# Reordering the opening of a convolution and attention kernel: loads, second-band inputs and the first phase's keys

## The chip, the core and the metric

The kernel runs on one core of a Trainium2 chip. Five engines work at the same time, each through its own instruction queue in the order of the program: PE (TensorE, matrix products and transposes), ACT (ScalarE, activation functions), DVE (VectorE), POOL (GpSimd) and SP (SyncE, which here only issues DMAs; ACT issues some as well). They wait for each other through semaphores. The metric is the device time of one execution in microseconds (us).

## What is computed

The input `x` has 4 images of 64 x 64 places with 128 channels, all in 32-bit floats. Two layers follow each other:

```python
c1  = conv3x3(elu(x), W1) + b1
c2  = conv3x3(c1, W2) + b2;  a, b = split(c2);  c3 = a * sigmoid(b)
# layer 0: one causal attention head over 4096 tokens, widths 4 and 16, tiled 8 times, then W3
x   = x + c3 + attention0(c3) @ W3 + b3
# layer 1: 16 heads of width 8 over the 4096 tokens, then a gated MLP (128 -> 344 -> 128)
t   = x + (h + ffn(h)),  h = n + attention1(n) @ wo,  n = layernorm(x)
# then 8 experts of 128 x 128, the best two mixed by their softmax weights
out = t + experts(layernorm(t))
```

The second attention is the bulk of the work: for each image and each of the 16 heads a 4096 x 4096 matrix of scores goes through the exponential.

## The kernel before, in words

An image's 4096 tokens are cut into 8 chunks of 512 (`NQ`), and keys into tiles of 128. The image is also seen as 4 bands of 16 rows, two chunks to a band. All engines are wrapped in `InOrder` (line 104), so each executes exactly in the order in which the Python code calls it. Every instruction is issued from line 114, so the profile shows that line everywhere and the groups are told apart by the names of their tiles.

**The stream.** After an opening in which the first image's convolutions begin, one long loop (line 1494) runs the second attention of all images. Each turn issues one step (line 922): 4 score products, 2 exponentials on ACT over 128 x 1024, and the products with the values. Between these the planner inserts pieces of other work, the fillers: the next chunks' and images' convolutions, first attention, layernorms, projections, and the MLP and experts of finished chunks. Fillers are Python generators; a turn usually advances one of them by one or two pieces, chosen from estimated costs.

**Phases of image 0.** The second attention needs keys of all chunks, so image 0 is done in three phases, with 2, 4 and 8 chunks of keys (line 1374). A phase runs over 4 groups of 4 heads; a pair of one group and one chunk of queries is a `Segment`. The first phase has 8 segments of 8 steps. A segment may start when `second`, the number of chunks whose operands are stored in DRAM, has reached the phase's number; otherwise the stream yields `None`, and the turn has no exponentials. Inside `stream` (line 1389), `bring` loads a run's values (`vg`) and a segment's queries (`qx`), for a follower already at the first step of the segment before it; `key_quarter` loads a quarter of a group's keys into one of 4 places in `kx` (the first phase uses place g for group g) and is called when a segment begins; `reload` refills a freed place for a later segment that is ready. A segment whose operands were not brought ahead is `late`: four turns of `None` precede it.

**The opening.** `run_alone` (line 1266) advances five generators in rounds, one piece of each per round, in this order: `convolutions` of image 0, `first_attention`, `second_operands_beside`, `fold_and_spread` (DVE) and `spread_beside` (POOL). The last two turn the 3 x 3 taps into Winograd form for later. Because that takes a while, bands 0 and 1 of image 0 are convolved directly by `first_bands` (line 489): `nine` issues 9 accumulated products per group of 8 rows, in three parts of 3 products, one part per round, all into one PSUM tile `m`. A band has two groups and a short one of a single row for the first layer, then for each of its two chunks a group for the value half and one for the gate half of the second layer; ACT finishes each group.

Their inputs come from `elu(n)` (line 546), which makes chunks up to number n: `neg` = exp on ACT, `pos` in two DVE instructions, a transpose on PE, and a DVE copy into `e_band`. It is a pipeline of three places, so k chunks take k + 2 pieces. Image chunks `xe` have two buffers: chunk n + 2 is loaded after chunk n has been read. `e_band` and `c_band` are two bands each, with a rim of zeros.

Before the rounds begin, line 226 loads the constants (the identity for the transposes among them), line 252 the first two image chunks, lines 253 to 263 the taps and biases on ACT's queue, lines 1289 and 1290 advance the convolution by five pieces, and then the other weights are loaded. Once `first_bands` has ended, `convolutions` makes the POOL terms `row_terms` and `col_terms` (lines 430 and 436; tile `r` shares one buffer with `taps2b`) for its Winograd part. `run_alone` stops when two chunks of second operands are stored, the taps are spread and `first_bands` is over. A layernorm (line 328) runs on DVE, except for its `rs`, a power on POOL.

Of the kernel before, what the change touches and what calls it, by code (L numbers as in the profile page):

```python
# [9 lines left out]
FP = mybir.dt.float32  # L10
FR = mybir.dt.float32r
AF = mybir.ActivationFunctionType
# [3 lines left out]
P = 128  # L16
# [110 lines left out]
def fast_path(ctx: ExitStack, tc: tile.TileContext, a: dict, where: dict, out: bass.AP, verdict):  # L127
# [95 lines left out]

    n_fast = where["tri"][1]
    consts = const.tile([P, n_fast], FP, name="f_consts")
    sp.dma_start(out=consts, in_=a["consts"][:, :n_fast])
    k_of = {name: consts[:, lo:hi] for name, (lo, hi) in where.items() if hi <= n_fast}
    ident = k_of["ident"]

# [3 lines left out]
    def load_x(b, c, tag):  # L233
        t = chunk(tag)
        sp.dma_start(out=by_k(t), in_=tb_x[b][:, 4 * c : 4 * c + 4, :])
        return t
# [8 lines left out]
    def taps(src, room=None):  # L245
# [3 lines left out]
            act.dma_start(out=t[:, i], in_=src[i].rearrange("kw i o -> i kw o"))  # L249
        return t  # L250

    first_x = [load_x(0, c, "xe") for c in range(2)]
    taps1 = taps(a["L0_conv_W1"])
    taps2a = taps(a["L0_conv_W2"][:, :, :, :C])
    b1 = const.tile([P, 1], FP, name="f_b1")
    act.dma_start(out=b1, in_=a["L0_conv_b1"].unsqueeze(1))
    b2 = const.tile([P, 2], FP, name="f_b2")
    act.dma_start(out=b2, in_=a["L0_conv_b2"].rearrange("(h p) -> p h", p=P))
    half_b2 = const.tile([P, 2], FP, name="f_half_b2")
    half_b2a = half_b2[:, 0:1]  # L260
    taps2b = taps(
        a["L0_conv_W2"][:, :, :, C:], row_tile()[:, : 9 * C].rearrange("p (i j o) -> p i j o", i=3, j=3)
    )


    v0 = const.tile([P, NT, SLOT], FP, name="f_v0")
# [8 lines left out]
    for band in (*e_band, *c_band):  # L275
        pool.memset(band[:, :, 0:1], 0.0)
        pool.memset(band[:, :, IMG + 1 :], 0.0)

    acc = ps_o.tile([P, QB], FP, tag="acc", name="acc")
    dve.memset(acc, 0.0)  # L280
    pool.tensor_scalar(half_b2, b2, 0.5, None, ALU.mult)

    seen = const.tile([P, 4, B], FP, name="f_seen")

# [204 lines left out]
    def first_bands(st, elu):  # L489


        def nine(taps, band, y, n):
            ps = rows(m_tile()[:, : n * IMG])
            for m in range(9):
                i, j = divmod(m, 3)
                pe.matmul(
                    ps,
                    lhsT=taps[:, i, j, :],
                    rhs=band[:, y + i : y + i + n, j : j + IMG],
                    start=m == 0,  # L500
                    stop=m == 8,
                )
                if m in (2, 5):
                    yield 0.0, "stop"
            return ps

        for r in range(2):
            here, there = e_band[r], e_band[1 - r]
            c_here = c_band[r]
            if r == 0:  # L510
                pool.memset(here[:, 0, :], 0.0)
                pool.memset(c_here[:, 0, :], 0.0)
            else:
                yield from elu(5)
                pool.tensor_copy(c_here[:, 0, :], c_band[0][:, 16, :])
            for band, y, n, to in (
                (here, 0, 8, slice(1, 9)),
                (here, 8, 8, slice(9, 17)),
                (there, 0, 1, slice(17, 18)),
            ):  # L520
                ps = yield from nine(taps1, band, y, n)
                act.activation(c_here[:, to, 1 : IMG + 1], ps, AF.Identity, bias=b1)
                yield 0.0, "stop"
            st.c3 = wk.tile([P, 2 * QB], FP, tag="c3", bufs=2, name="c3")
            for h in range(2):
                c3, gate = st.c3[:, h * QB : (h + 1) * QB], chunk("sd", "gate")
                ps = yield from nine(taps2a, c_here, 8 * h, 8)
                act.activation(rows(c3), ps, AF.Identity, bias=half_b2a, scale=0.5)
                yield 0.0, "stop"
                ps = yield from nine(taps2b, c_here, 8 * h, 8)  # L530
                act.activation(rows(gate), ps, AF.Tanh, bias=half_b2[:, 1:2], scale=0.5)
                dve.scalar_tensor_tensor(c3, gate, 1.0, c3, ALU.add, ALU.mult)
                st.done.append(c3)
                yield 0.0, "stop"
        st.plain = False

    def tiles(ap):
# [725 lines left out]

    batches = []

    def run_alone(gens, until):

        gens, last = list(gens), {}
        while gens and not (until() and "rounds" not in last.values()):
            for gen in list(gens):  # L1270
                r = next(gen, None)
                while r is not None and r[1] == "held":
                    r = next(gen, None)
                last[gen] = r and r[1]
                if r is None:
                    gens.remove(gen)
                if steps_in:
                    do_step(steps_in.pop(0))
                    finish(1)
                elif undone:  # L1280
                    finish(0)
        while steps_in:
            do_step(steps_in.pop(0))
        finish(0)
        return gens

    Batch(0)

    for _ in range(5):
        next(batches[0].conv)  # L1290

    def weight(name, src, shape):
        w = const.tile(shape, FP, name="f_" + name)
# [92 lines left out]
    jobs = []  # L1386
    now, quiet = [0], [False]

    def stream():
        in_kx, vg_of = [None] * 4, {}  # L1390
        ahead = {}

        def key_quarter(seg, quarter):
            place, what = seg.place(quarter), (seg.b, seg.g, quarter)
            if in_kx[place] != what:
                keys(scratch[seg.b], seg.g, quarter, place)
                in_kx[place] = what

        def bring(seg):

            if seg.run not in vg_of:
                vg_of.clear()
                vg_of[seg.run] = values_of(scratch[seg.b], seg.g, seg.n)
            ahead[seg] = queries(scratch[seg.b], seg.g, seg.c), vg_of[seg.run]

        def reload(at, seg, quarter):

            for later in plan[at + 1 :]:
                quarters = [q for q in range(later.lo // 8, later.hi // 8) if later.place(q) == seg.place(quarter)]
                if quarters:  # L1410
                    if later.ready():
                        key_quarter(later, quarters[0])
                    break

        for at, seg in enumerate(plan):
            now[0] = seg.b
            while not seg.ready():
                yield None
            late = seg not in ahead
            if late:  # L1420
                bring(seg)
            qx, vg = ahead.pop(seg)
            part = []
            for quarter in range(seg.lo // 8, seg.hi // 8):
                key_quarter(seg, quarter)
            for _ in range(4 if late else 0):
                yield None
            follower = plan[at + 1] if at + 1 < len(plan) else None
            over = []
            for kt in range(seg.lo, seg.hi):  # L1430
                if kt in seg.beside:
                    continue
                if kt == seg.lo + 2:
                    seg.jobs = [Beside(seg, n, qx, vg) for n in range(len(seg.beside))]
                    jobs[:] = seg.jobs
                steps_left[seg.b] -= 1

                quiet[0] = kt < seg.lo + 2 and at > 0 and not late
                if seg.lo > 0 and kt == seg.lo + 4:

                    part.append(chunk("part"))
                    sp.dma_start(out=part[0], in_=scratch[seg.b]["p"][seg.g, seg.c])
                yield attention_step(seg.b, seg, kt, 8 * seg.place(kt // 8) + kt % 8, qx, vg, part)
                if follower and follower not in ahead and follower.ready():
                    bring(follower)
                if kt % 8 == 7:
                    over.append(kt // 8)
                if not any(job.kt // 8 in over and job.units < NSLOT for job in seg.jobs):
                    for quarter in over:
                        reload(at, seg, quarter)  # L1450
                    over.clear()
            for job in seg.jobs:
                while job.units < NSLOT:
                    while bank_held[0]:
                        insert()
                    beside_work(1e9)
                    job.piece()
            for quarter in over:
                reload(at, seg, quarter)
# [14 lines left out]
    def spread_beside():  # L1474
# [5 lines left out]
    left = run_alone(  # L1480
        [st.conv, first_attention(0, st), second_operands_beside(0, st), fold_and_spread(), spread_beside()],
        lambda: st.second >= plan[0].n and len(spread_of) == 3 and not st.plain,
    )
    alone[0] = False

# [790 lines left out]
```

## Time and profile before

| What | Value |
|---|---|
| Runs of the kernel | 7969.11, 7976.05, 7983.45 us; median 7976.05 |
| The profiled execution | 7979.66 us, of it 7977.8 us between its first and last instruction (the span) |
| Granted PE clock, mean over the span | 0.992 |
| DMA traffic | 360.96 MB, mean 45 GB/s |

The profile describes one execution. Its page gives busy times by engine, the span in 40 slices of 199 us with the busy share in tenths, and the costliest groups. The timeline lists instructions in order of time, neighbours of one kind merged: start, duration, engine, line, operation, the tile written and the tiles read, the count, and in brackets the idle time of the engine before it with what ended it. `SPq` and `ACTq` are DMA issues. Windows give the busy time of each engine in chosen stretches. The columns of the next lines are the window, its length, busy times with instruction counts, the granted PE clock, the DMA share and GB/s:

```profile
0.00:20.00 20.00, 3.35 (x12) 2.15 (x12) 5.57 (x13) 3.06 (x4) 3.52 (x28) 1.00 0.66 165
20.00:40.00 20.00, 18.24 (x36) 7.59 (x36) 10.57 (x15) 0.69 (x1) 16.07 (x17) 1.00 0.45 116
...
80.00:100.00 20.00, 9.54 (x47) 4.83 (x45) 11.67 (x39) 1.72 (x3) 1.38 (x3) 0.86 0.00 0
100.00:120.00 20.00, 18.53 (x74) 9.82 (x74) 14.38 (x29) 3.88 (x5) 0.00 (x0) 0.79 0.35 121
...
180.00:200.00 20.00, 10.96 (x108) 5.68 (x108) 12.77 (x35) 5.71 (x6) 1.18 (x2) 0.74 0.26 94
200.00:220.00 20.00, 19.28 (x216) 7.35 (x216) 6.00 (x11) 19.65 (x23) 0.00 (x0) 1.00 0.20 62
```

The busy times stand in the order PE, PE weight loads, DVE, ACT, POOL. From 200 us on ACT is busy nearly all the time; before, PE is, except in the first window, from 80 to 100 and from 180 to 200.

### The profile page before, as it was taken

The numbers are of one execution on the slowest core, as the hardware profiler recorded it, in microseconds if no ns is written. First come the engines' busy times: TensorE is split into PE (matmuls) and PEld (weight loads), VectorE is DVE, ScalarE is ACT, GpSimd is POOL, SyncE is SP. The second block draws the span as 40 slices with busy tenths as digits, with TensorE's granted clock in tenths as the row PEclk, the third lists the DMA queues.
The fourth block names the chain that finished last, engine by engine and source line by source line (L and its number), as shares of the span: only waits on it lengthen the run. The fifth ranks groups of instructions, "written<-read, shape, count | busy, mean of one in ns | idle before, by whom it ended". The sixth has DMA issues, their size and how long they took to land.

```text
span 7977.8 us, 237947 instructions
## 1 busy us (share of the span) xinstructions
PE 7760.0 (97%) x103701; PEld 3280.2 (41%) x103701; DVE 4798.3 (60%) x9289; ACT 7661.9 (96%) x8459; POOL 671.5 (8%) x592
## 2 busy tenths in 40 slices
PE   7899999999999999999999999999999999999998
PEld 3333444444444444444444444444444333333334
DVE  4333556462666776666666776666666666666664
ACT  1899999999999999999999999999999999999996
POOL 1201211000022100000001210000000000000000
PEclk9999999999999999999999999999999999999998
DMA  2222011111110111111010011111111111111221
GB/s 71 70 68 69 23 60 33 60 41 53 35 34 15 50 39 50 38 31 43 25 41 29 19 43 43 51 42 34 33 29 52 50 49 53 50 54 50 70 73 38
DMA packets 334834, 360.96 MB, mean 45 GB/s; under 512 B 148211, under 2 KB 224467, under 8 KB 333779
## 3 DMA queue, kind: packets, MB, share of 16 engines
q1 hardware_dynamic: 329763, 343.87, 13.6%
q8 instruction: 814, 13.34, 0.7%
q10 hardware_dynamic: 4016, 1.77, 0.1%
q14 instruction: 241, 1.97, 0.1%
HBM read 209.50 MB, written 136.05 MB: 43 GB/s over the span
## 4 chain that ended last, share of the span: by engine, by line
PE 44%; issue 2%; DVE 2%; ACT 2%; DMA 0%; POOL 0%; SPq 0%; ACTq 0%; DVEq 0%; POOLq 0%
PE acc L114 22%; PE s L114 13%; PE m L114 9%; ACT e L114 1%; DVE ey L114 1%; DVE h L114 0%; DVE em L114 0%; DVE t L114 0%; DVE eg L114 0%; DVE by_e L114 0%; DMA blocks<-d_y 0%; SPq L114 0%; POOL rs L114 0%; DVE f_c_band L114 0%; DVE c L114 0%
## 5 line engine op out<-in xcount | busy, mean ns | idle before, releaser
L114 ACT ACTIVATE e<-s 128x1024 f32<-128x1024 f32 x8256 | 7600.4, 1113 | 111.2 <-PE s L114 106.6
L114 PE MATMUL acc<-e,vg 128*9 128x128 f32 (+3 forms) x61880 | 4278.8, 387 | 1.9 <-DVE at L114 1.8
L114 PE MATMUL s<-qx,f_kx 32*128 32x512 f32 (+1 forms) x16512 | 2556.8, 495 | 88.7 <-ACT e L114 56.4
L114 PEld LDWEIGHTS acc<-e,vg 128*9 128x9 f32 x61880 | 1562.0, 90 | 1777.6 <-issue 1209.5
L114 PEld LDWEIGHTS s<-qx,f_kx 32*128 32x128 f32 (+1 forms) x16512 | 1049.1, 182 | 2068.4 <-ACT e L114 1337.7
L114 DVE SCALAR_TENSOR_TENSOR ey<-ey,eg 128x512 f32<-128x512 f32 x1344 | 940.2, 700 | 31.9
L114 DVE COPY at<-acc 128x512 f32<-128x512 f32 x131 | 90.6, 691 | 597.9 <-PE acc L114 593.4
L114 PE MATMUL m<-v,f_wino 128*32 128x256 f32 x5376 | 420.2, 391 | 12.0 <-POOL v L114 7.3
L114 DVE TENSOR_SCALAR ey<-m 128x512 f32<-128x512 f32 x448 | 307.6, 687 | 89.8 <-PE m L114 80.0
L114 DVE SCALAR_TENSOR_TENSOR eg<-em,ey 128x512 f32<-128x512 f32 x448 | 316.7, 707 | 11.4
L114 DVE SCALAR_TENSOR_TENSOR ey<-ey,em 128x512 f32<-128x512 f32 x448 | 316.7, 707 | 9.5
L114 POOL TENSOR_TENSOR rs<-ve,f_minus_half 128x4 f32<-128x4 f32 x64 | 65.3, 1020 | 3027.4 <-DVE ve L114 2995.0
L114 DVE SCALAR_TENSOR_TENSOR ey<-eg 128x512 f32<-128x512 f32 x448 | 312.7, 698 | 0.0
L114 POOL TENSOR_TENSOR v<-r 128x1024 f32<-128x1024 f32 x112 | 219.1, 1962 | 975.4 <-PE m L114 975.0
L114 DVE COPY sd<-m 128x512 f32<-128x512 f32 x168 | 116.0, 690 | 301.5 <-PE m L114 301.1
L114 PE MATMUL m<-f_we,y2T 128*32 128x256 f32 x3968 | 291.9, 388 | 0.0
L114 DVE TENSOR_TENSOR by_e<-m,gates 128x512 f32<-128x512 f32 x248 | 170.3, 687 | 176.7 <-PE m L114 175.5
L114 PE MATMUL m<-hT,f_fw 128*32 128x256 f32 (+1 forms) x2728 | 233.0, 390 | 1.3 <-DVE hT L114 1.2
L114 POOL TENSOR_TENSOR t<-t,h 128x512 f32<-128x512 f32 x32 | 44.5, 1391 | 2240.6 <-DVE h L114 2240.6
L114 DVE TENSOR_TENSOR t<-m,t 128x512 f32<-128x512 f32 x61 | 42.2, 692 | 308.9 <-PE m L114 308.8
L114 DVE TENSOR_SCALAR em<-ey 128x512 f32<-128x512 f32 x448 | 200.4, 447 | 13.7
L114 DVE TENSOR_SCALAR em<-em 128x512 int32<-128x512 int32 x448 | 196.1, 438 | 10.0
(260 smaller groups left out, 4381.3 us busy)
## 6 DMA issues: line engine op xcount, KB each, us to landing
f_kx<-d_k SPq DMA_DIRECT2D x139, 512.0 KB
qx<-d_q SPq DMA_DIRECT2D x152, 256.0 KB
d_q<-two SPq DMA_DIRECT2D x64, 512.0 KB
d_a<-at SPq DMA_DIRECT2D x128, 256.0 KB
vg<-d_v SPq DMA_DIRECT2D x32, 576.0 KB
d_k<-two SPq DMA_DIRECT2D x32, 512.0 KB
d_v<-vc SPq DMA_DIRECT2D x32, 288.0 KB
xe<-in_x_dram SPq DMA_DIRECT2D x32, 256.0 KB
```

Source lines behind the costliest of these rows:

```text
L114: made = op(*args, **kw)
```

## The change

It has four parts, all in the opening.

1. A one-column activation is the first thing on ACT, before its DMAs. The first image chunk is loaded ahead of the constants, the second behind them. Only the first layer's taps are issued before the convolution is advanced by three pieces; the second layer's taps and the biases follow, then two more pieces.
2. The zero rows of `e_band[0]` and `c_band[0]` are written at the start and no longer inside `first_bands`.
3. In `first_bands`, a band's second-layer groups are each followed by one piece of `elu`, for the next two chunks: chunks 3 and 4 in band 0, chunks 5 and 6 in band 1. The `elu(5)` that stood between the bands goes; the `elu(7)` after them finds nothing left to do.
4. `run_alone` gets a function that it calls once, at the start of a round, when two chunks of second operands are stored: it asks for the first segment's queries and loads the key quarter of every segment of the first phase, which is one quarter for each of the four groups. The first segment is then no longer `late`.

```diff
-    sp.dma_start(out=consts, in_=a["consts"][:, :n_fast])
...
-    first_x = [load_x(0, c, "xe") for c in range(2)]
+    warm = const.tile([P, 1], FP, name="f_warm")
+    dve.memset(warm, 0.0)
+    act.activation(warm, warm, AF.Exp)
+    first_x = [load_x(0, 0, "xe")]
+    sp.dma_start(out=consts, in_=a["consts"][:, :n_fast])
+    first_x.append(load_x(0, 1, "xe"))
     taps1 = taps(a["L0_conv_W1"])
-    taps2a = taps(a["L0_conv_W2"][:, :, :, :C])
...
+    pool.memset(e_band[0][:, 0, :], 0.0)
+    pool.memset(c_band[0][:, 0, :], 0.0)
...
-            if r == 0:
-                pool.memset(here[:, 0, :], 0.0)
-                pool.memset(c_here[:, 0, :], 0.0)
-            else:
-                yield from elu(5)
+            if r == 1:
                 pool.tensor_copy(c_here[:, 0, :], c_band[0][:, 16, :])
...
             st.c3 = wk.tile([P, 2 * QB], FP, tag="c3", bufs=2, name="c3")
+            inputs = elu(5 + 2 * r)
             for h in range(2):
                 c3, gate = st.c3[:, h * QB : (h + 1) * QB], chunk("sd", "gate")
                 ps = yield from nine(taps2a, c_here, 8 * h, 8)
                 act.activation(rows(c3), ps, AF.Identity, bias=half_b2a, scale=0.5)
+                next(inputs, None)
                 yield 0.0, "stop"
                 ps = yield from nine(taps2b, c_here, 8 * h, 8)
                 act.activation(rows(gate), ps, AF.Tanh, bias=half_b2[:, 1:2], scale=0.5)
                 dve.scalar_tensor_tensor(c3, gate, 1.0, c3, ALU.add, ALU.mult)
                 st.done.append(c3)
+                next(inputs, None)
                 yield 0.0, "stop"
+            yield from inputs
...
-    def run_alone(gens, until):
+    def run_alone(gens, until, first=None):
...
         while gens and not (until() and "rounds" not in last.values()):
+            if first and batches[0].second >= plan[0].n:
+                first()
+                first = None
...
-    for _ in range(5):
+    for _ in range(3):
         next(batches[0].conv)
+    taps2a = taps(a["L0_conv_W2"][:, :, :, :C])
...
+    taps2b = taps(
+        a["L0_conv_W2"][:, :, :, C:], row_tile()[:, : 9 * C].rearrange("p (i j o) -> p i j o", i=3, j=3)
+    )
+    for _ in range(2):
+        next(batches[0].conv)
+    pool.tensor_scalar(half_b2, b2, 0.5, None, ALU.mult)
...
+    def ask_first():
+
+        ask(plan[0])
+        for seg in plan:
+            if seg.n == plan[0].n and seg.b == 0:
+                key_quarter(seg, 0)
...
-            late = seg not in ahead
-            if late:
+            late = seg not in brought and seg not in asked
+            if seg not in brought:
                 bring(seg)
-            qx, vg = ahead.pop(seg)
+            qx, vg = brought.pop(seg)
...
     left = run_alone(
         [st.conv, first_attention(0, st), second_operands_beside(0, st), fold_and_spread(), spread_beside()],
         lambda: st.second >= plan[0].n and len(spread_of) == 3 and not st.plain,
+        ask_first,
     )
```

`key_quarter` and `bring` are as before, moved out of `stream`; `ask` is the query half of the former `bring`, which now takes the queries from there.

More of the change, by code (lines that the diff above doesn't have):

```diff
@@ L250, in taps @@
         return t
-    first_x = [load_x(0, c, "xe") for c in range(2)]
-    taps1 = taps(a["L0_conv_W1"])
-    taps2a = taps(a["L0_conv_W2"][:, :, :, :C])
[L255 to L263, printed above, removed]
+    warm = const.tile([P, 1], FP, name="f_warm")
[4 more added lines that the diff above has]
+    first_x.append(load_x(0, 1, "xe"))
+    taps1 = taps(a["L0_conv_W1"])
     v0 = const.tile([P, NT, SLOT], FP, name="f_v0")
@@ L277, in fast_path @@
         pool.memset(band[:, :, IMG + 1 :], 0.0)
+    pool.memset(e_band[0][:, 0, :], 0.0)
+    pool.memset(c_band[0][:, 0, :], 0.0)
     acc = ps_o.tile([P, QB], FP, tag="acc", name="acc")
     dve.memset(acc, 0.0)
-    pool.tensor_scalar(half_b2, b2, 0.5, None, ALU.mult)
     seen = const.tile([P, 4, B], FP, name="f_seen")
@@ L1287, in fast_path @@
     Batch(0)
-    for _ in range(5):
+    for _ in range(3):
         next(batches[0].conv)
+    taps2a = taps(a["L0_conv_W2"][:, :, :, :C])
+    b1 = const.tile([P, 1], FP, name="f_b1")
+    act.dma_start(out=b1, in_=a["L0_conv_b1"].unsqueeze(1))
+    b2 = const.tile([P, 2], FP, name="f_b2")
+    act.dma_start(out=b2, in_=a["L0_conv_b2"].rearrange("(h p) -> p h", p=P))
+    half_b2 = const.tile([P, 2], FP, name="f_half_b2")
+    half_b2a = half_b2[:, 0:1]
+    taps2b = taps(
[4 more added lines that the diff above has]
+    pool.tensor_scalar(half_b2, b2, 0.5, None, ALU.mult)
     def weight(name, src, shape):
@@ L1387, in fast_path, with key_quarter, ask, bring @@
     now, quiet = [0], [False]
-    def stream():
[L1390 to L1404, printed above, removed]
+    in_kx, vg_of = [None] * 4, {}
+    brought, asked = {}, {}
+    def key_quarter(seg, quarter):
+        place, what = seg.place(quarter), (seg.b, seg.g, quarter)
+        if in_kx[place] != what:
+            keys(scratch[seg.b], seg.g, quarter, place)
+            in_kx[place] = what
+    def ask(seg):
+        if seg not in asked:
+            asked[seg] = queries(scratch[seg.b], seg.g, seg.c)
+    def bring(seg):
+        if seg.run not in vg_of:
+            vg_of.clear()
+            vg_of[seg.run] = values_of(scratch[seg.b], seg.g, seg.n)
+        ask(seg)
+        brought[seg] = asked.pop(seg), vg_of[seg.run]
+    def ask_first():
[3 more added lines that the diff above has]
+                key_quarter(seg, 0)
+    def stream():
         def reload(at, seg, quarter):
@@ L1443, in stream @@
                 yield attention_step(seg.b, seg, kt, 8 * seg.place(kt // 8) + kt % 8, qx, vg, part)
-                if follower and follower not in ahead and follower.ready():
+                if follower and follower not in brought and follower.ready():
                     bring(follower)
```

## The prediction

> **What bounds the kernel now.** First the page, then the timeline of the opening 200 us, then windows and waits around the first attention phase. All times are of the profiled execution.
>
> ```profile
> PE 7760.0 (97%) x103701; PEld 3280.2 (41%) x103701; DVE 4798.3 (60%) x9289; ACT 7661.9 (96%) x8459; POOL 671.5 (8%) x592
> ACT  1899999999999999999999999999999999999996
> L114 ACT ACTIVATE e<-s 128x1024 f32<-128x1024 f32 x8256 | 7600.4, 1113 | 111.2 <-PE s L114 106.6
> ```
>
> The 8256 exponentials hold ScalarE for 7600.4 us, 0.92 us each when back to back; their number does not change. The span is therefore this sum plus ScalarE's idle time. It is 316 us (7977.8 - 7661.9), more than half of it in the first of the 40 slices. What the change is worth is how much earlier the stream of exponentials starts, and which of its holes close. PE, 97% busy, is filled up to ScalarE's time by the planner, so a hole that closes gives back its whole width.
>
> The timeline at the places that matter (start, duration, engine, what, idle before):
>
> ```profile
> 8.73 1.28 ACT L114 ACT_TABLE_LOAD   x1 [8.73 <-DMA taps<-in_L_conv_W_dram]
> 20.77 0.16 POOL L114 MEMSET f_e_band<- 128x66 f32 x1
> 20.98 10.62 PE L114 MATMUL m<-f_e_band,taps 128*128 128x512 f32 x18 [4.88 <-POOL f_e_band L114]
> ...
> 87.31 0.69 ACT L114 ACTIVATE gate<-m,f_half_b 128x512 f32<-128x512 f32 x1 [10.82 <-PE m L114]
> 100.25 1.09 PE L114 MATMUL s<-f_consts,pos 128*128 128x128 f32 x4 [9.12 <-DVE pos L114]
> 109.67 2.74 PE L114 MATMUL m<-f_e_band,taps 128*128 128x512 f32 x6
> ...
> 178.42 0.69 ACT L114 ACTIVATE gate<-m,f_half_b 128x512 f32<-128x512 f32 x1 [7.04 <-PE m L114]
> 193.51 3.77 ACT L114 ACTIVATE e<-s 128x1024 f32<-128x1024 f32 x4 [13.89 <-PE s L114]
> ```
>
> Until 178 us the chain is PE's nine-tap products (one 512-column group is 7.99 us in three parts of 2.74). It begins at 20.98, behind a 0.16 us memset that POOL's queue reached late; it stops from 87.31 to 109.67, where four rounds make the second band's inputs; and after the last gate the stream needs 15.1 us to start. Inside the stream, in its first phase:
>
> ```profile
> 232.21 0.51 PE L114 MATMUL s<-qx,f_kx 32*128 32x512 f32 x4 [1.91 <-issue]
> 267.16 0.80 PE L114 MATMUL s<-qx,f_kx 32*128 32x512 f32 x4 [5.55 <-DMA f_kx<-d_k]
> 303.70 0.80 PE L114 MATMUL s<-qx,f_kx 32*128 32x512 f32 x4 [5.82 <-DMA f_kx<-d_k]
> ```
>
> Each is the first product of a head group (1, 2, 3) waiting for keys issued 4.5, 6.5 and 7.2 us before.
>
> **Part A: the start.** Before, ScalarE issued 11 DMAs from 0.74 to 8.71 (0.72 us each), loaded its table and ran the first `neg` at 10.03. After: table load at about 0.74 (1.28 us), the warm activation, three tap issues (2.2 us) until 4.4. The image chunk now goes first on SP; DMA traffic was saturated from 2.5 to 10.5 (about 290 GB/s), and 256 KB ahead of the rest land by about 4. `neg` of chunks 0 and 1 then run at about 4.4 and 5.5. The other eight issues (5.9 us) stand between `neg` 1 and `neg` 2 on ScalarE's queue: `neg` 2 at about 12.0, against 13.58. From there as before: the DVE pair to 13.3, PE's transposes 13.4 to 14.5, and the first product follows at once, for the zero row is no longer queued behind the weights' bias work. 20.98 becomes 14.5: **6.5 us**, plus 0.5 for a PE that is already active (six passes of the first group ran at 0.86 instead of 0.43 us). The moved memsets (2 x 0.16) and the warm column lie in POOL's and DVE's empty first 5 us; without that cover they cost 0.4 us. The scaling of `b2` waits for its DMA (about 11.5) with only POOL's weight copies behind it, whose own data land at about 16.
>
> **Part B: second band's inputs between the first's products.** Chunks 3 and 4 add two PE transposes (0.66 each) before 87.31. One stands in PE's queue, **-0.7**; the other fills the 1.59 us in which PE waits for the gate. DVE's added pairs (1.1 us) lie where it waits for products (1.29 idle at 65.04 and 90.01), and SP's image loads move ahead of loads needed 20 us later. In return the four rounds between 87.31 and 109.67 (22.4 us, PE busy 11.6) now carry four product parts. Followed along PE: query product to 90.0; part, key and value products, part, transposes, part to 99.8 (before, PE stood still 9.12 here); then scores, exponentials, masks and values of chunk 1 with the same waits as before, about 7 us to 106.7; the fourth part and a 0.5 us product to 110.0. That is the state of 109.67 with four parts (11.0 us) done: **10.7 us**. Chunks 5 and 6 in the second band cost one exposed transpose, **-0.7**. Rounds fall from 48 to 44. Sum so far: 6.5+0.5-0.7+10.7-0.7 = 16.3; the last gate moves from 178.4 to **162.1**.
>
> **Part C: the stream's start.** Four turns without exponentials (10.5 us, 182.1 to 192.6) go, since the first segment's queries are asked for early. After the gate come the query product, second operands, key and value products (3.0 us before), then scores; the first exponential could run about 4 us after the gate instead of 15.1. But something else is late next: the conv's next step is no longer ELU but the row and column terms on POOL, and they enter POOL's queue ahead of the `rs` of chunk 2's layernorm.
>
> ```profile
> 188.13 1.02 POOL L114 TENSOR_TENSOR rs<-ve,f_minus_half 128x4 f32<-128x4 f32 x1 [40.30 <-DVE ve L114]
> ...
> 255.02 4.91 POOL L114 TENSOR_TENSOR r<-f_e_band 128x528 f32<-128x528 f32 x4 [28.66 <-DVE f_e_band L114]
> 260.00 7.98 POOL L114 TENSOR_TENSOR v<-r 128x1024 f32<-128x1024 f32 x4
> ```
>
> They share their buffer with the second layer's taps, so they start at the gate and hold POOL 12.9 us; `rs` was needed 9.7 us after it. Behind `rs` wait `h` on DVE, then its transposes on PE (third turn), and behind these all later scores. By rows alone: `rs` at gate+13, `h` to 15.3, PE free at 16. The Trainium skill (SBUF — State Buffer, Who interferes with whom) speaks against overlapping further: a DVE instruction with two SBUF inputs or in a two-port mode is blocked for the whole of a GpSimd instruction that reads SBUF. About eight such instructions stand before `rs`; at up to one 1.96 us `v` each that is +16 us, `rs` at gate+26. The trace is milder: four `h` took 2.13 us beside a POOL add and 1.11 without, and `pos` 1.06 against 0.42, so 0.3 to 0.6 each; I take 0.6, +5 us, `rs` at gate+15. Then the fourth step's exponentials start about gate+19 = 181.1, against 200.3: the lead is 19.2 us, so C brings **2.9** net. Ends: no block, fourth step at gate+12, lead 26; the rule in full, gate+30, lead 8.
>
> **Part D: keys of the first phase.** All four groups' quarters (4 x 512 KB) are issued when chunk 1's keys are stored, some 30 us before the stream; group 0's already ran early before (145.71), so it gains nothing, but the holes of groups 1 to 3 go. On ScalarE these are 1.67, then 4.77 and 0.62, then 6.07, 1.05 and 0.19: **14.4 us**. SP is moved past nothing urgent: image loads 5 to 7 wait on ELU in front of stores that nobody needs soon. Query and value loads were already one segment ahead. Ends: 10 (value loads late next) to 14.4.
>
> **Sum.** 19.2 + 14.4 = 33.6 us. Against the profiled run (7979.66, span 7977.8) that gives 7946; its neighbour runs have the median 7976.05, 3.6 lower, and I take it from there: **7942**.
>
> **What else could happen.**
> - *Likeliest (0.55):* as summed, 7930 to 7955 by the ends of C and D.
> - *DVE becomes the bound of the second band (0.20).* For: 11.67 and 14.38 busy of 20 us from 80 to 120, without a gap from 88 to 100. Against: `pos` leaves that stretch, and the products need no DVE result there. Then of the 10.7 only two transposes (2.2) remain: gain 25, 7951.
> - *POOL does not hold the stream back (0.12).* Were layernorm's `rs` one round earlier, the gain is 26 + 14.4: 7936.
> - *The early keys do not arrive early (0.07)*, SP standing at an image load: 19 us remain, 7957.
> - *Slower (0.06): the second phase ends before the eighth chunk is ready.* The planner's fillers set this: chunk 7's keys were stored at 742.10 and the third phase's queries asked for at 743.37, in the phase's last turns. A missed turn costs 2.6 us (10.5/4), and a miss brings four more. Fillers lose three turns (the four that went) and gain four (ELU of chunks 5 and 6 and the terms, done earlier), so I expect one turn of advance. To lose all 33.6 us plus the 9.8 us key wait there needs 13 turns missed, or a replan that doubles the 41.5 us of holes from 1000 to 7840: about 7990.
>
> **Range and chances.** 7929 to 7964 leaves out the slow case and the outer ends. 0.2% is 16 us, what the measurement can tell from no change. Faster by more takes the first three cases and over half of the fourth, less some doubt for the replanned rest: 0.84; within: 0.10; slower: 0.06.
>
> **What will show it.** First product near 14.5 with no POOL release; no PE gap of 9 us before the second band; last gate near 162; a POOL `v` run of 8 us straight after it, then `rs` and a ScalarE hole of 5 to 8 us at the third or fourth step; no key waits at groups 1 to 3. Wrong if the gate is past 170, if these holes reappear at value loads, or if turns without exponentials stand near 720.

## The result and the profile after

| | Before | After |
|---|---|---|
| Median of 5 runs each | 7981.15 us (7969.11 to 7983.45) | 7943.24 us (7937.72 to 7944.53) |
| Ratio, 95% interval | | 0.9955 (0.9940 to 0.9969) |
| Profiled execution, its span | 7979.66, 7977.8 us | 7943.24, 7941.4 us |

The kernel became 37.9 us faster by the medians (two more runs of the kernel before raised its median from 7976.05), 25 to 48 us by the interval of the ratio, and 36.4 us by the two profiled executions. 7942 was predicted, and the range of 7929 to 7964 holds the result. Several of the terms behind it were off all the same, in both directions.

From the page of the kernel after: busy times, the row of ScalarE in 40 slices, and its costliest group.

```profile
PE 7753.8 (98%) x103661; PEld 3284.0 (41%) x103661; DVE 4804.7 (61%) x9290; ACT 7662.2 (96%) x8460; POOL 671.3 (8%) x592
ACT  2999999999999999999999999999999999999996
L114 ACT ACTIVATE e<-s 128x1024 f32<-128x1024 f32 x8256 | 7600.8, 1118 | 85.6 <-PE s L114 79.8
```

The exponentials cost 7600.8 us, as before (7600.4). ScalarE's idle time fell from 316 to 279 us (7941.4 - 7662.2), and of the 37 us some 26 stand directly before exponentials (111.2 to 85.6). Only the first two slices changed, from 1 to 2 and from 8 to 9. So the work is the same and the stream starts earlier and with fewer holes, as the prediction read it.

The timeline of the kernel after at the places that the prediction named (start, duration, engine, what, idle before; lines come from several stretches):

```profile
0.74 1.28 ACT L114 ACT_TABLE_LOAD   x1 [0.74 <-PEq L2285]
13.27 10.21 PE L114 MATMUL m<-f_e_band,taps 128*128 128x512 f32 x18
...
35.70 7.96 PE L114 MATMUL m<-f_c_band,taps 128*128 128x512 f32 x18 [0.45 <-issue]
...
78.03 0.69 ACT L114 ACTIVATE gate<-m,f_half_b 128x512 f32<-128x512 f32 x1 [10.82 <-PE m L114]
...
94.50 2.84 PE L114 MATMUL m<-f_e_band,taps 128*128 128x512 f32 x6
98.05 2.74 PE L114 MATMUL m<-f_e_band,taps 128*128 128x512 f32 x6
...
155.24 0.69 ACT L114 ACTIVATE gate<-m,f_half_b 128x512 f32<-128x512 f32 x1 [7.04 <-PE m L114]
159.93 1.03 ACT L114 ACTIVATE e<-s 128x1024 f32<-128x1024 f32 x1 [4.01 <-PE s L114]
```

The first product no longer has a release by POOL in its brackets; it follows the transposes without a gap, at 13.27 instead of 20.98. The state of 109.67 before is reached at 98.05, and four product parts are done by then (by 83.3, 86.6, 89.6 and, the one at 94.50, 97.3). The last gate is at 155.24 instead of 178.42, and the stream's first exponential follows 4.7 us later instead of 15.1.

To place gains I use the **lead**: the start of the n-th exponential in the kernel before minus its start in another kernel, each from its own span's start; for other instructions it is the same difference:

| Place | Predicted lead | Measured lead |
|---|---|---|
| first nine-tap product; first `f_c_band` | 6.5; 7.0 | 7.7; 8.1 |
| gate of chunk 1 | 6.3 | 9.3 |
| last gate of the second band | 16.3 | 23.2 |
| ninth exponential of the stream (past its first holes) | 19.2 | 23.1 |
| behind the key holes of groups 1 to 3 | 33.6 | 39.1 |
| third phase under way | 33.6 | 40.0 |
| last exponential | 33.6 | 36.1 |

### The profile page after: what moved, and what is told of

Read it like the earlier page. It is cut to its first block, busy times and chain, and to the rows that moved or that the text cites. A ratio compares the mean times of both kernels' runs of the same rounds, so it can differ in the third digit from the quotient of the medians.

```text
span 7941.4 us, 237872 instructions
## 1 busy us (share of the span) xinstructions
PE 7753.8 (98%) x103661; PEld 3284.0 (41%) x103661; DVE 4804.7 (61%) x9290; ACT 7662.2 (96%) x8460; POOL 671.3 (8%) x592
## 4 chain that ended last, share of the span: by engine, by line
PE 44%; issue 2%; DVE 2%; ACT 2%; DMA 0%; POOL 0%; SPq 0%; ACTq 0%; DVEq 0%; POOLq 0%
PE acc L114 22%; PE s L114 13%; PE m L114 9%; ACT e L114 2%; DVE ey L114 1%; DVE h L114 0%; DVE em L114 0%; DVE t L114 0%; DVE eg L114 0%; DVE by_e L114 0%; POOL rs L114 0%; ACT th L114 0%; DVE f_c_band L114 0%; DVE c L114 0%; DMA blocks<-d_y 0%
## 5 line engine op out<-in xcount | busy, mean ns | idle before, releaser
L114 ACT ACTIVATE e<-s 128x1024 f32<-128x1024 f32 x8256 | 7600.8, 1118 | 85.6 <-PE s L114 79.8
```

The lines of the kernel that those rows point to most:

```text
L114: made = op(*args, **kw)
```

## The experiments

Each kernel was timed over five rounds beside runs of the kernel before on the same chip; the difference is between the medians of that set.

| Experiment | Median us | Before us | Difference | Ratio, 95% interval |
|---|---|---|---|---|
| start only | 7971.19 | 7979.99 | -8.8 | 0.9983 to 0.9999 |
| second-band inputs only | 7973.12 | 7979.99 | -6.9 | 0.9983 to 0.9999 |
| early keys only | 7975.01 | 7979.99 | -5.0 | 0.9986 to 1.0003 |
| terms after the layernorm | 7941.03 | 7979.99 | -39.0 | 0.9940 to 0.9967 |
| early keys, late turns kept | 7965.02 | 7980.48 | -15.5 | 0.9972 to 0.9988 |
| after, without early keys | 7958.32 | 7980.48 | -22.2 | 0.9960 to 0.9982 |
| after, places turned | 7938.69 | 7980.48 | -41.8 | 0.9935 to 0.9962 |
| places turned and terms later | 7933.32 | 7980.48 | -47.2 | 0.9927 to 0.9954 |
| after, without part 4 | 7961.24 | 7982.06 | -20.8 | 0.9965 to 0.9984 |
| zero rows only | 7973.18 | 7982.06 | -8.9 | 0.9983 to 0.9996 |

The intervals are 10 to 22 us wide, so differences of a few us are not settled by the times; there the traces are read. A trace is one execution, too: up to the last gate, experiments 4 and 5 below leave the work of PE and ScalarE as it was, and their traces lead by 2.1 and 1.8 us there all the same, so a lead of some 2 us settles nothing. The changed kernel's own set has 7943.24 beside 7981.15; the medians of the kernel before in the four sets lie within 2.1 us. Experiments 6 to 10 are compared with the changed kernel across sets and carry that doubt as well.

**1. The start alone.** The kernel before with parts 1 and 2 of the change.

> The kernel before with parts 1 and 2 of the change alone (order of the loads, warm activation, zero rows at the start). The sum: PE's first product at 13 to 15 us instead of 20.98, the gate of chunk 1 about 8 to 9.5 us earlier, and the whole of it reaches the end: 8 to 9.5 us faster than the kernel before. Rival (the start is hidden: weights or taps that land late hold the later groups up anyway): under 3 us. The key waits of groups 1 to 3 and the 9 us gap before the second band stay in the trace.

The first product starts at 13.39, and the lead is 9.0 us at the last gate. It shrinks to between 3.5 and 5.2 in the holes of the first two phases and is 9.5 at the last exponential. The gain, 8.8 us, and the first gate, 9.5 us earlier, are as the theory has them; why some 5 us go and come back was not traced.

**2. The zero rows alone.** The kernel before with only this:

```diff
+    pool.memset(e_band[0][:, 0, :], 0.0)
+    pool.memset(c_band[0][:, 0, :], 0.0)
...
-            if r == 0:
-                pool.memset(here[:, 0, :], 0.0)
-                pool.memset(c_here[:, 0, :], 0.0)
-            else:
+            if r == 1:
```

> The kernel before with only the zero rows moved ahead of the input copies on GpSimd. Theory: the first nine-tap product is released by the transposes' copies instead of the zero rows and starts near 16.2 us instead of 20.98, and the time falls by 4.5 to 5 us; the table load and the tap issues hold the rest of the start's 8.8 us. Rival (the start waits for the ScalarE exponential as well as for the zero rows, so that both must move): the first product stays above 19 us and the time falls by less than 2 us.

PE's timeline of this kernel:

```profile
14.97 1.12 PE L114 MATMUL s<-f_consts,pos 128*128 128x128 f32 x4 [1.43 <-DVE pos L114]
15.88 8.84 PE L114 MATMUL m<-f_e_band,taps 128*128 128x512 f32 x18
```

The product starts at 15.88, 5.1 us earlier, straight behind the transposes. Two memsets of 0.16 us, moved past the weight work in POOL's queue, are thus two thirds of the 7.6 us that experiment 1 gained at this place; the loads' order and the table, which were not run apart, bring the other 2.5. The time fell by more than the 5.1 us, but 5 lies within the interval (3 to 14 us), and the lead in the trace, 6.0 at the stream's start and 8.1 at the end, says no more about the start.

**3. The second band's inputs alone.** The kernel before with part 3.

> The kernel before with part 3 alone (inputs of chunks 3 to 6 made between the products). The sum: the 9.12 us gap of PE at 100 us goes, the last gate comes 12 to 14 us earlier than 178.4; but the row and column terms now stand on POOL ahead of the layernorm's rs, so the first exponential of the stream comes 18 to 21 us after that gate instead of 15.1, and about 5 us are given back: 7 to 10 us faster than before. Rival (DVE bounds the second band, the products wait for it wherever they stand): the last gate 2 to 4 us earlier, and with the POOL wait 0 to 3 us slower than before.

The last gate is at 162.83, 15.6 us earlier, but ScalarE's timeline shows what follows:

```profile
162.83 0.69 ACT L114 ACTIVATE gate<-m,f_half_b 128x512 f32<-128x512 f32 x1 [7.04 <-PE m L114]
183.57 3.77 ACT L114 ACTIVATE e<-s 128x1024 f32<-128x1024 f32 x4 [20.05 <-PE s L114]
```

The stream begins 20.7 us after the gate, where it took 15.1 before: the row and column terms on POOL now come ahead of the layernorm, and the late turns are still there. The lead drops from 15.6 to 9.9 at this place. PE's longest wait in the second band is 1.59 us, so DVE did not become its bound, the rival to which 0.20 was given. The gate came earlier than the 12 to 14 us expected (1.7 of the 15.6 us are there at the first band's last gate already, which was to come no earlier), and the time, 6.9 us, ended just under the expected 7 to 10.

**4. The early keys alone.** The kernel before with part 4.

> The kernel before with part 4 alone (first queries and four key quarters early, no late turns). The sum: the ScalarE holes of groups 1 to 3 go (15 to 16 us as the two traces have them), and the stream starts about 5 us after the last gate with a short wait for the layernorm at its third turn, 7 to 9 us ahead of before: 22 to 25 us faster. Rival (the planner's fillers, four turns further behind, are not ready when the second phase ends): turns without exponentials near 740 us, and at most 14 us faster.

This is the rival. The lead is 21.8 us once the key holes are past, and stays there up to the end of the second phase; then it falls to 4.2. ScalarE and a DMA issue of SP in this kernel, around the start of the third phase:

```profile
722.01 1.94 ACT L114 ACTIVATE e<-s 128x1024 f32<-128x1024 f32 x2
...
732.03 0.52 SPq L114 DMA_DIRECT2D d_k<-two  x1
...
743.80 0.63 ACT L114 ACTIVATE neg<-xe 128x512 f32<-128x512 f32 x1 [19.85 <-DMA xe<-in_x_dram]
...
747.45 0.63 ACT L114 ACTIVATE neg<-xe 128x512 f32<-128x512 f32 x1 [2.22 <-DMA xe<-in_x_dram]
747.98 5.60 ACT L114 ACTIVATE e<-s 128x1024 f32<-128x1024 f32 x6
```

The second phase's last exponentials end at 723.95, but the eighth chunk's keys are stored (`d_k`) only at 732.03. The next exponential starts at 747.98. That is 24 us without one, where the kernel before had 9.8: the place and the cause that the prediction's slow case named, with a price of 14 us more. The last stretch is not a wait for keys by itself: the late turns have put three inputs of a later convolution ahead of the new phase, and in ScalarE's in-order queue their `neg` wait for image loads until 747.45, right before the exponentials. PE likewise waits 17.51 us, until 745.30, for such an input ahead of its first scores.

**5. The early keys with the late turns kept.** As 4, but the first segment's queries are not asked for ahead, so its four turns without exponentials remain:

```diff
     def ask_first():
-        ask(plan[0])
         for seg in plan:
```

> The kernel before with the four early key quarters alone; the queries are not asked for early, so the four late turns stay and with them four filler pieces before the stream. If the keys-only run lost its gain because the fillers were four turns behind, then here the holes of groups 1 to 3 go, the stream starts as before, the boundary of the second and third phase has its old hole of about 10 us (not 20), and the kernel is 11 to 16 us faster than before, although it has less of the change than the keys-only run (5 us). Rival (early keys cost something later by themselves, such as their DMA traffic or SP's order): the 20 us hole near 740 stays and the gain is under 6 us.

15.5 us, with the lead at 15.8 behind the key holes and constant through the third phase's start, where the hole is 10.03. It differs from 4 by the four turns alone. So leaving the four turns out is worth 8 us of lead at the ninth exponential and 6 behind the key holes, and costs 17 at the end of the second phase, when nothing else makes the fillers earlier.

**6. The changed kernel without the early keys.** The inverse, `ask(plan[0])` kept and the loop over `plan` left out.

> The changed kernel with the first segment's queries asked for early but no keys. The sum: the holes of groups 1 to 3 come back and nothing else moves, 13 to 17 us slower than the changed kernel (7956 to 7960 where that one has 7943). Rival (the keys are hidden by other waits at those places): under 6 us slower.

15.1 us slower than the changed kernel (7958.32 against 7943.24, in another set; by the differences within each set, 15.7). The two ways of measuring part D's keys agree, at 15.5 and 15.1.

**7. The changed kernel without part 4.** Parts 1 to 3 together.

> The changed kernel with its fourth part undone: the first phase's keys are asked for in the late turns again, after the sixth and seventh chunk. Theory (the parts are independent at the start and in the second band, and add there; the fourth part is worth its 15 us of keys only because the third part has moved as many filler steps ahead of the stream as the fourth takes out of the late turns): the two gains seen alone add up, 8.8 + 6.9 = 15.7 us below the kernel before, so 7962 to 7967, and the fourth part is worth 20 to 23 us beside the third where it was worth 5 alone; the third phase starts with a hole near 9.8 us. Rival (the third part's own gain is hidden until the keys are early, so that the parts overlap): 8 to 11 us below the kernel before, near 7970. Second rival (the start and the second band gain more together than apart): 18 us or more, 7962 or less.

20.8 us: by the numbers set down, this is the second rival, more together than apart, though the interval of the ratio, 13 to 28 us, holds the sum of 15.7 as well. The trace shows where an excess would lie. At the ninth exponential the lead is 16.8, against 7.7 + 9.5 = 17.2 for parts 1 and 2 and part 3 alone, so at the start the gains do add up. The excess comes later: nothing is lost in the key holes here (18.4 behind them, where the two alone had 4.9 and 7.8), and the third phase's start brings more than 4: the hole there is 4.75 us, not the expected 9.8. Part 3 alone has 4.85 there, and parts 1 and 2 alone 9.96. Part 4 beside the other three is worth 7961.24 - 7943.24 = 18.0 us, less than the 20 to 23 expected, but far more than the 5.0 alone.

**8. The terms after the layernorm.** The changed kernel, with one empty step ahead of the row and column terms of image 0:

```diff
             yield from elu(7)
+            yield 0.0, "stop"
```

> The changed kernel with one more yield ahead of the row and column terms of image 0, so that they are issued with chunk 4 and POOL has rs of chunks 2 and 3 ahead of them. If POOL's queue holds the stream's fourth step back, the ScalarE hole of 7.56 us at 168 to 176 shrinks to 1 to 3 us and the kernel is 4 to 8 us faster than the changed kernel (about 7936 to 7939 where that one has 7943). Rival (DVE's own chain of second operands sets h, and POOL only stands beside it): the hole keeps over 5 us and the time is that of the changed kernel within 2 us.

Two lines of this kernel's timeline, from POOL and ScalarE, stand against those of the changed kernel:

```profile
164.45 1.02 POOL L114 TENSOR_TENSOR rs<-ve,f_minus_half 128x4 f32<-128x4 f32 x1 [29.31 <-DVE ve L114]
169.80 1.94 ACT L114 ACTIVATE e<-s 128x1024 f32<-128x1024 f32 x2 [4.36 <-PE s L114]
```

```profile
155.28 5.17 POOL L114 TENSOR_TENSOR r<-f_e_band 128x528 f32<-128x528 f32 x4 [21.37 <-PE m L114]
160.52 8.05 POOL L114 TENSOR_TENSOR v<-r 128x1024 f32<-128x1024 f32 x4
170.60 1.02 POOL L114 TENSOR_TENSOR rs<-ve,f_minus_half 128x4 f32<-128x4 f32 x1 [2.03 <-DVE ve L114]
...
175.95 1.94 ACT L114 ACTIVATE e<-s 128x1024 f32<-128x1024 f32 x2 [7.56 <-PE s L114]
```

`rs`, the layernorm's power, comes 9.7 us after the gate (154.74 in this kernel), as before the change, and no longer 15.4. Its brackets in the changed kernel tell why it was late there: POOL had been done for 2.03 us, and `rs` waited for `ve` from DVE. So POOL's queue did not hold it to the end. The terms slowed DVE's chain ahead of it (the lines are in the next section). The hole at the stream's fourth step falls from 7.56 to 4.36, between the 1 to 3 expected and the over 5 of the rival. The lead at the ninth exponential is 7.0 us larger (30.1 against 23.1). The time is only 2.2 us shorter, below the 4 to 8 expected and within the noise. Of the 7.0 us over the changed kernel 3.7 are left at 226 us, behind the place where the terms now stand beside the next chunk's layernorm, 1.4 behind the third phase's start, and 0.6 at the end. That the terms' place makes `rs` late is shown; the gain was mostly lost again later.

**9. The places of the keys turned.** The hole of 9.8 us at the third phase's start is the same in both kernels and is a wait for keys: their places are in use until the second phase ends. In the changed kernel, the second phase is made to end on other places, and a quarter is reloaded as soon as its own chunks are stored:

```diff
-                    base = (0, g, 2 * (g % 2), 0, 0)[n // 2]
+                    base = (0, (g + 2) % 4, 2 * ((g + 1) % 2), 0, 0)[n // 2]
...
-                    if later.ready():
+                    if len(batches) > later.b and batches[later.b].second >= 2 * (quarters[0] + 1):
```

> The changed kernel with the key places of image 0's first and second phase turned by two, so that the second phase's last group leaves places 2 and 3 free, and a freed place refilled as soon as the two chunks of its quarter are stored, not all eight. The third phase's first keys then land long before it starts. The ScalarE hole of 9.78 us at the start of the third phase (705 to 715) shrinks to 2 to 4 us, which the queries then set; 5 to 8 us faster than the changed kernel. Rival (queries and values of the third phase, issued at the same moment, land as late as the keys): the hole keeps over 8 us and the time stays within 2 us.

4.6 us faster than the changed kernel, a little less than the 5 to 8 expected. The timelines of PE and ScalarE, first of the changed kernel, then of this one:

```profile
714.13 0.80 PE L114 MATMUL s<-qx,f_kx 32*128 32x512 f32 x4 [10.04 <-DMA f_kx<-d_k]
715.02 1.94 ACT L114 ACTIVATE e<-s 128x1024 f32<-128x1024 f32 x2 [9.78 <-PE s L114]
```

```profile
708.97 0.80 PE L114 MATMUL s<-qx,f_kx 32*128 32x512 f32 x4 [4.72 <-DMA qx<-d_q]
709.86 1.94 ACT L114 ACTIVATE e<-s 128x1024 f32<-128x1024 f32 x2 [4.47 <-PE s L114]
```

The hole halves, to just above the 2 to 4 expected. What is left is a wait for queries, 4.72 us at the product ahead of it.

**10. Both.** The edits of 8 and 9 together.

> The last one with the row and column terms after the layernorm as well. If what that edit gave back came from the start of the third phase, both gains stand: 4 to 7 us faster than the places alone. Rival (the filler piece that it moves into the stream is given back later wherever it goes): within 3 us of the places alone.

7933.32 us, 5.4 below 9 and 9.9 below the changed kernel. It is the fastest of all versions tried.

## Why the prediction was right, and where it was not

**The bound** was read rightly: ScalarE's busy time did not move, and what the opening gained came back nearly in full in the span (lead 39.1 behind the key holes, 36.4 between the spans).

**Part A (7.0)** measured 8.1. The table load is at 0.74 as predicted. The 1.1 us come from ScalarE: the eight issues that stand between the second and the third `neg` took 4.1 us instead of 5.9, so `neg` of the third chunk is at 10.96 instead of the predicted 12.0, although the second image chunk landed late and its `neg` ran at 6.83, not 5.5.

**Part B, first band (-0.7)** measured +1.2. The transpose is in PE's queue as predicted. What the sum did not have is the group that follows the short row group: 7.96 us after, 9.43 before, with a granted clock of 1.00 and 0.84 in the windows around it. All ten experiments show 7.96 or 7.97, also 3, 4 and 5, whose start is as before. The 1.5 us are therefore a slower moment of the one profiled execution before, and no gain of the change.

**Part B, second band (10.7 - 0.7)** measured 13.9. PE's gap of 9.12 us is gone, all four parts stand where they were put, and the stretch from scores to values took 5 us (89.55 to 94.50) where I took 7 from before. The prediction overlooked why it was 7: after the gap PE ran at half rate. Its granted clock was 0.50 from 100 to 108 us in the kernel before, and 1.00 from 86 to 98 in the kernel after. The values' products show it, before and after:

```profile
104.78 3.59 PE L114 MATMUL acc<-e,f_v 128*32 128x512 f32 x16
```

```profile
92.14 2.44 PE L114 MATMUL acc<-e,f_v 128*32 128x512 f32 x16
```

So the gap had cost more than its width. Counted from the gate, the state of 109.67 came 2.7 us sooner than summed; the other 1.2 us of this part lie behind it and were not traced. (Two readings of the prediction here are off and change nothing: PE was busy for 10.7 of the 22.4 us, not 11.6, and DVE's idle times of 1.29 and 1.15 us lie between 88 and 100, where none was seen.)

**Part C (+2.9)** is the step that failed in size: -0.1. The prediction had the right thing late next, `rs` once the terms stand on POOL, and put it at gate+15; it came at gate+15.4. POOL's queue alone would have let it go when POOL was done, at 168.57 or gate+13.3; what came last was DVE's chain. Here the rule that the prediction cites can be weighed against its own figure of 0.6 us for each DVE instruction. DVE's timeline in the kernel after, then the same instructions before, where POOL stood still:

```profile
160.77 2.29 DVE L114 SCALAR_TENSOR_TENSOR qx<-u,f_consts,w 128x512 fp32r<-128x512 f32 x1
163.37 0.61 DVE L114 SCALAR_TENSOR_TENSOR xt<-s,rs,xt 128x128 f32<-128x128 f32 x2
165.21 1.57 DVE L114 TENSOR_SCALAR w<-u,f_consts 128x128 fp32r<-128x128 f32 x1
166.81 1.91 DVE L114 SCALAR_TENSOR_TENSOR f_kx<-u,f_consts,w 128x128 fp32r<-128x128 f32 x1
```

```profile
183.02 0.75 DVE L114 SCALAR_TENSOR_TENSOR qx<-u,f_consts,w 128x512 fp32r<-128x512 f32 x1
184.07 0.61 DVE L114 SCALAR_TENSOR_TENSOR xt<-s,rs,xt 128x128 f32<-128x128 f32 x2
185.58 0.28 DVE L114 TENSOR_SCALAR w<-u,f_consts 128x128 fp32r<-128x128 f32 x1
185.89 0.35 DVE L114 SCALAR_TENSOR_TENSOR f_kx<-u,f_consts,w 128x128 fp32r<-128x128 f32 x1
```

Three instructions are longer by 1.54, 1.29 and 1.56 us; with 0.49 for `c`, 0.44 for the first `w` and 0.34 for `f_v` that is 5.66, and the way from gate to `rs` grew by 5.65 (9.71 to 15.36). The sum of 5 was right, but not by eight delays of 0.6 us: three long ones make 4.4 of it, and that it came out right is luck. On this stretch the Trainium skill's rule (SBUF — State Buffer, Who interferes with whom), that the engine which issues second is blocked until the other's instruction ends, describes the three better than my 0.6 did. `xt`, whose input `s` is in PSUM, kept its 0.61 beside `v`, as the rule has it. The +16 was too high because I charged every candidate a whole `v`, where the three lost 1.3 to 1.6 us each and the others less than 0.5; by the rule each waits for what is left of the one `v` that it meets.

What C lacked lies behind `rs`. From there to the fourth step's exponentials I allowed 4 us; it took 5.4 (170.60 to 175.95), so they came at gate+20.7 instead of +19. PE's timeline:

```profile
172.06 1.24 PE L114 MATMUL m<-f_consts,h 128*128 128x128 f32 x4 [5.56 <-DVE h L114]
173.23 1.90 PE L114 MATMUL acc<-e,vg 128*9 128x512 f32 x8
```

PE came back from its wait at half rate: the window of 172 to 179 us has a granted clock of 0.55, and its value products and scores took 1.90 and 0.80 us, against 1.04 and 0.51 at full clock, which is 1.2 us. The trace before had shown the same at this place (0.50 from 190 to 196 us, after a wait of 7.58), and the prediction left it out. The next step still ran slowly and left the hole of 1.16 ahead of 179.05. So the fourth step came 1.7 us later after the gate than summed, and the ninth exponential another 1.3: the 3.0 that C missed.

**Part D (14.4)** measured 16.0, and 15.5 and 15.1 in experiments 5 and 6. No key wait is left in groups 1 to 3: ScalarE runs 64 exponentials from 179.05 and, behind one `neg`, 94 more from 237.74 without a wait between them, where waits of 1.67, 4.77 and 6.07 us stood before. The result lies above the upper end of 14.4; what the other 1.6 us are was not taken apart. The value loads did not come late.

**The slow case (0.06)** did not happen, and experiments 4 and 5 show how close it was. Part 4 takes four turns from the fillers (the prediction counts three, though it names the four that went); part 3 gives them four pieces, the ELU of chunks 5 and 6 and the terms, done before the stream starts. That part 3, and not the earlier start, makes up for part 4 is argued from this count and from the hole at the third phase's start, which part 3 halves without part 4 and parts 1 and 2 do not; no run has part 4 with one of them alone. Alone, part 4 was late for the third phase and kept 4.2 of 21.6 us of lead; beside part 3 it kept its lead (40.2 before that place, 40.0 behind it). The place was right. The price was the turns missed and four more at 2.6 us each; the 17.4 us lost are six to seven such turns. How many were missed the trace does not count, so the price per turn stays open; the waits for image loads in experiment 4 are not in it.

**Not predicted** were the 3 us lost behind the third phase's start, nearly all between the exponential that began at 5808 us before (lead 39.9) and the end (36.1). 2.2 of them are lost at one place, where ScalarE waits 2.90 us (until 7771.48) and before 1.12; PE there had waited 2.53 us, before 1.50, for a tile that comes by DMA. Experiment 7 loses 1.3 in this stretch; experiment 10 loses 1.4, and 3.9 in the stretch ahead of it. The five runs of the two kernels spread over 14 us before and 7 after, so this may be no property of the change; its cause stays open.

The errors of the sum are 6.9 too little at the last gate, 3.0 too much in C, 1.6 too little in D and 3.0 lost late, together the 2.5 between 33.6 and 36.1. The step of 3.6 us from the profiled execution to the median was not borne out by further runs. That the forecast came within 2 us is therefore partly luck.

## What to carry to other kernels

Price a chain from gate to gate, but look also for what now enters a queue early: when work moves ahead, it runs beside other work than before (here POOL's terms slowed DVE), and a wait of the matrix engine cost its clock as well (0.50 for 6 to 8 us behind waits of 5.56 and 9.12). Do not add up or take apart edits that move work through a planner: the fourth part was worth 5 us alone and 18 beside the others, because what was ready 550 us later decided. And look first for small instructions at the end of a long in-order queue: two memsets of 0.16 us held the first product for 5 us.

## What the runs showed of the hardware

- After 5.56 us without work on PE, its granted clock was 0.50 from 172 to 178.4, for 6.4 us of nearly unbroken work; in the kernel before, after a gap of 9.12 us, it was 0.50 from 100 to 108. The Trainium skill (TensorE: Matmul & The Clock Gate, Part 1) has the full clock come back after at least one busy window of some 3.4 us; these traces show about twice that.
- The same 18 products of the very first group took 10.62 us before, 10.21 after and 8.84 with the zero rows alone, and 9.0 to 10.4 in the seven kernels with the new start; 18 such products at full rate take 7.99.
- DMA issues on ScalarE took 0.5 us each after the change (three in 1.51, 1.46 and 1.56 us), where the eleven in a row before it took 0.72 each.
- Beside POOL's 2 us additions a DVE instruction of 128 x 128 elements took up to 1.91 us instead of 0.35, while `xt`, with one of its two operands in PSUM, kept its 0.61.
